# A four-layer graph network on one core: narrow sums of two turn pairs together, and the closing sums and products in another order

## The chip, the core and the metric

The kernel runs on one core of a Trainium2 chip. The time is that of the device in microseconds, from the first to the last instruction of one execution. Three runs of the kernel before gave a median of 811.44 us (811.31 to 813.11).

## What is computed

The input is a feature matrix `x` of 4096 nodes by 64, and a dense adjacency `adj` of 4096 by 4096 whose entries are 0 or 1 (about one in 128 is 1). Four layers follow each other, and each adds its result to `x`:

```
h = relu(layernorm(x));  x = x + layer_k(h, adj)      for k = 0, 1, 2, 3
```

Layer 0 weighs the neighbours of a node by their rank from the end, w = 0.5 ** (number of later neighbours), up to 100 of them, and computes `w @ (h @ W) + b`. Layer 1 is an attention with weights `adj * sigmoid(score)`. Layer 2 is a gated unit applied twice, each time with `m = adj @ (x @ W)`. Layer 3 is a weighted midpoint on a hyperbolic ball:

```
num = A @ (gamma * X);  den = A @ (gamma - 1);  alpha = sum(A, axis=1)
two_mean = num / den;   mid = tanh(0.5 * artanh(|two_mean|)) * direction
out = tanh(alpha * artanh(|mid|)) * direction        -> logmap, relu, expmap
```

## The kernel before, in words

**Tiling.** The nodes are 32 blocks of 128. The transposed adjacency is cut into four column quarters q of 1024, and so into 128 tiles of 128 x 1024. Each is loaded once, as one byte per entry, and kept for all layers (`A8`, names A...). Most are cast by the DMA that GpSimd issues (`load0`, L860), some come whole in float32 and are cast on chip (`cast0`). The program assumes that all entries are 0 or 1, and so every tile is loaded whole a second time, at whatever moment, and tested on VectorE (`checks`: `whole` with the sum of odd entries in `odd`). At the end one product of 128 x 1 (`flag_ps`) adds up what was found; where something was, a general kernel runs after this one. In this case it doesn't.

**Who sets the order.** The kernel is written as generators that yield operations, and a planner, `Weave`, issues them while the program is built. It keeps a clock for each engine (`self.t`), a cost for each operation (for instance 0.2 + 0.9e-3 n us on ScalarE, in `Engine.cost`), and the time at which each tile will be ready. The main streams (`stream0`, `stream1`, `layer2`, `layer3`) write TensorE's products in a fixed order. At each `weave.draw()` the planner puts in what fits from the waiting pieces: preparation of the next layer (`pre0` ... `pre3`, `post0` ... `post3`), and, as a background piece, the entry tests. While `weave.quiet` holds, no background piece is drawn. The engines then run what they were given, each in its own order; whatever the planner's clocks say, on the chip they wait by semaphores.

**Layer 0** (`stream0`). A turn takes one tile (block b, quarter q), b downwards from 31. `turn` multiplies the tile by a triangular matrix (`ftri`), after the earlier tile was multiplied by another one (`fupd`), and so keeps in two accumulator banks, `cnt0` and `cnt1` of 512 columns each, the number of later neighbours of each entry. ScalarE or VectorE reads each bank into `w` (times -128, relu, as int16: read as bfloat16 that is the weight). The first bank is always read by ScalarE, the second by ScalarE in turns of even b, by VectorE in turns of odd b from the twelfth turn on. The next turn's first product may go into a bank when it has been read. Two turns make a pair, and a pair's sums (`sums`) come two pairs or so later:

```
first turn | three wide sums | second turn | one wide sum, four narrow sums
```

The source of the sums, `h`, is split in three bfloat16 parts: two of them stand side by side in `hm` (128 columns, wide), the third in `lo` (64 columns, narrow: `add_lo`). A narrow sum uses one column half of the array; the sums for c = 0 and c = 1 use different halves.

**Layer 3** (`layer3`). The source `S3` is split in three parts again, so that one product of 128 x 196 gives all of them (`sum3`). The 4096 result nodes are eight parts u of 512. Accumulators have room for three parts, so parts 0, 1, 2 are first summed over the first half of the source blocks and set aside (`take3`), then 3, 4, 5 over all of them, in four quarters as the source gets ready; then the second half of 0, 1, 2; then 6 and 7. `post3` closes three parts at a time (6 and 7 singly): signs, lengths, artanh, tanh, relu, addition to `X`, store. It works on VectorE and ScalarE beside the sums. In its closing `between()` scales v by relu and the reciprocal length (names n<-n,ny in the profile), while the logarithm is computed; the result of tanh (rc) then scales v once more (n<-n,rc).

Of the kernel before, what the change touches and what calls it, by code (L numbers as in the profile page):

```python
# [13 lines left out]
ALU = mybir.AluOpType  # L14
# [555 lines left out]
NQ = 4  # L570
QB = 8
# [220 lines left out]
def fast_kernel(ctx: ExitStack, tc: tile.TileContext, t: dict, out: bass.AP, flag: bass.AP):  # L792
# [13 lines left out]
    NB = N // P  # L806
# [10 lines left out]
    weave = Weave()  # L817
# [314 lines left out]
    def stream0():  # L1132

        cols = [slice(c * CW, (c + 1) * CW) for c in (0, 1)]
        cnt, acc, waiting = [], {}, []

        def turn(q, b):

            n = q * NB + NB - 1 - b
            a = a8(q, b)  # L1140
            weave.at[A8[q][b // 2].tensor.name] = weave.at[A8[q][b // 2].tensor.name + "odd" * (b % 2)]
            wt = b2("w", (P, 2 * CW), I16)
            for c in (0, 1):
                if b < NB - 1:
                    before = a8(q, b + 1)(c)
                    mm(like(cnt[c], before), upd, before, start=False, stop=False)
                mm(like(cnt[c], a(c)), tri, a(c), start=b == NB - 1, stop=b == 0)

                if c == 0 or b % 2 == 0 or n < 12:
                    S_.activation(wt[:, cols[c]], cnt[c], AF.Relu, scale=-128.0)  # L1150
                else:
                    V.tensor_scalar(wt[:, cols[c]], cnt[c], -128.0, 0.0, op0=ALU.mult, op1=ALU.max)
            if n + 12 < len(tiles) and not direct(n + 12):
                load0(n + 12)
            if n + 12 < len(tiles) and direct(n + 12):
                load0(n + 12)
            for k in (1, n + 3):
                if k in whole:
                    cast0(k)
            return [wt[:, x].bitcast(BF16) for x in cols]  # L1160

        def sums():

            if not waiting:
                return
            q, b, w0, w1 = waiting[0]
            if b == NB - 1:
                acc[q] = [one(f"acc{c}") for c in (0, 1)]
            for c in (0, 1):
                add_hm(acc[q], 0, b, c, w0[c], b == NB - 1)  # L1170
            add_hm(acc[q], 0, b - 1, 0, w1[0], False)
            yield
            add_hm(acc[q], 0, b - 1, 1, w1[1], False)
            for i, wt in enumerate((w0, w1)):
                for c in (0, 1):
                    add_lo(acc[q], 0, b - i, c, wt[c], b - i == 0)
            waiting.pop(0)
            if b == 1:
                weave.add(post0(q, acc.pop(q)))

        def here(item):
            part = source(0, item[1])[0]
            return part in DONE and weave.ready("P", names(LO[part])) <= weave.t["P"]

        for q in range(NQ):
            cnt[:] = [two(f"cnt{c}")[:, :CW] for c in (0, 1)]
            for b in range(1, NB, 2)[::-1]:

                if len(waiting) > 3:
                    weave.until(source(0, waiting[0][1])[0], DONE)  # L1190
                first = second = iter(())
                if waiting and (len(waiting) > 3 or here(waiting[0])):
                    first = second = sums()
                w0 = turn(q, b)
                weave.draw()
                next(first, None)
                weave.draw()
                w1 = turn(q, b - 1)
                weave.draw()
                next(second, None)  # L1200
                weave.draw()
                waiting.append((q, b, w0, w1))
                if q == 0 and b in (NB - 1, NB - 3):
                    load_x((b - NB + 3) // 2, S_)
                    weave.add(pre0((b - NB + 3) // 2))
                if q == 0 and b == NB - 3:
                    weave.add(checks(), back=True)
                if q == 0 and b == NB - 9:
                    S_.dma_start(W, t["consts"][:, :L.at["scales"].stop])
                    weave.add(constants())  # L1210
                if len(waiting) > 2 and here(waiting[0]):
                    for _ in sums():
                        weave.draw()
                if b == NB // 2 + 1:
                    load_x(q, Y_)
                    if q == 0:
                        depth[0] = 2
                    if q == NQ - 1:
                        load1(0)
                        depth[0] = 2  # L1220
            for x in cnt:
                free(x)
        begin1()
        while waiting:
            for _ in sums():
                weave.draw()
# [459 lines left out]
    def layer3():  # L1686

        half = NB // 2
        sets = (0, 1, 2), (3, 4, 5)
        early = {}  # L1690
        for k in range(2):
            for place, u in enumerate(sets[0]):
                weave.until((4, k), DONE)
                sum3(u, place, k * QB, k * QB + QB)
                if k:
                    early[u] = take3(u)
        for lo, hi in ((0, 1), (1, 2), (2, 3), (3, 4)):
            for place, u in enumerate(sets[1]):
                weave.until((4, lo), DONE)
                sum3(u, place, lo * QB, hi * QB)  # L1700
                if hi == NQ:
                    summed(u, take3(u))
        weave.quiet = False
        while weave.back and weave.back[0][1].e == "D":
            weave.issue(weave.back[0])
        for place, u in enumerate(sets[0]):
            sum3(u, place, half, NB)
            summed(u, take3(u, early.pop(u)))
        for place, u in enumerate((6, 7)):
            sum3(u, place, 0, NB)  # L1710
            summed(u, take3(u), alone=True)
        while weave.back:
            weave.force(True)
        others = nc.values_load(flag)
        weave.finish()
        return others
# [31 lines left out]
    def post3(parts3):  # L1748

        nb = CB * len(parts3)
        sgn, den, ss = stat("sgn", nb), stat("den", nb), stat("ss", 2 * nb)
        part = [slice(i * CB, (i + 1) * CB) for i in range(len(parts3))]
        vs = [n65[:, :, :D] for u, (n65, al) in parts3]
        for h, v, (u, (n65, al)) in zip(part, vs, parts3):
            d = n65[:, :, D]
            yield DV.tensor_scalar(sgn[:, h], d, 0.0, 2.0, op0=ALU.is_ge, op1=ALU.mult)  # L1760
            yield DV.scalar_tensor_tensor(v, rows(sgn[:, h]), -1.0, v, op0=ALU.add, op1=ALU.mult)
            sq = b2("sq")
            yield AC.activation(sq[:, :CB, :], v, AF.Square)
            yield DV.scalar_tensor_tensor(sq[:, CB:, :], v, 0.0, v, op0=ALU.max, op1=ALU.mult)
            yield DV.tensor_scalar(den[:, h], d, -1.0, DEN_EPS, op0=ALU.mult, op1=ALU.max)
            yield DV.tensor_tensor(den[:, h], den[:, h], d, ALU.max)
            yield DV.tensor_reduce(ss.rearrange("p (k b) -> p k b", k=2)[:, :, h],
                                   sq.rearrange("p (k b) d -> p k b d", k=2), AX.X, ALU.add)
        yield from preload(AF.Ln)
        rd = yield from recip(den)  # L1770
        n, r = yield from lengths(ss)
        t = stat("t", nb)
        yield DV.tensor_tensor(t, n[:, :nb], rd, ALU.mult)
        ratio = stat("ratio", nb)

        def between():
            yield DV.tensor_tensor(ratio, n[:, nb:], r[:, :nb], ALU.mult)
            for h, v in zip(part, vs):
                yield DV.scalar_tensor_tensor(v, v, 0.0, rows(r[:, nb:][:, h]), op0=ALU.max, op1=ALU.mult)

        a = yield from artanh2(t, between())
        for h, (u, (n65, al)) in zip(part, parts3):
            yield DV.scalar_tensor_tensor(a[:, h], a[:, h], 0.25, al, op0=ALU.mult, op1=ALU.mult)
        yield DV.scalar_tensor_tensor(a, a, ARTANH_MAX, ratio, op0=ALU.min, op1=ALU.mult)
        yield AC.activation(a, a, AF.Tanh)
        for h, v, (u, (n65, al)) in zip(part, vs, parts3):
            yield DV.tensor_tensor(v, v, rows(a[:, h]), ALU.mult)
            x = X[u // 2][:, (u % 2) * CB:(u % 2 + 1) * CB, :]
            yield DV.tensor_tensor(x, x, v, ALU.add)
            yield SY.dma_start(out_nm[:, u * CB:(u + 1) * CB, :], x)  # L1790
# [103 lines left out]
```

## Time and profile before

| stretch, us | stage | TensorE busy | VectorE busy | ScalarE busy |
|---|---|---|---|---|
| 5 to 232 | layer 0 | 220.1 | 168.5 | 132.9 |
| 232 to 493 | layer 1 | 257.6 | 216.4 | 166.9 |
| 493 to 695 | layer 2, both steps | 200.2 | 167.1 | 53.3 |
| 695 to 790 | layer 3 with sums | 94.6 | 72.3 | 35.5 |
| 790 to 811 | closing without sums | 0.0 | 13.3 | 7.1 |
| whole span, 810.7 | | 772.4 (95%) | 638.3 (79%) | 396.9 (49%) |

A row of the profile gives the engine, the line, the operation, the names written and read (buffer numbers left out), the shape and how often. Nearly all lines are those of two helpers (L781 for VectorE, ScalarE and the DMA issues of the sync queue, L976 for products), so the names tell what it is: cnt is a count bank, acc an accumulator, hm and lo the source parts, whole an entry test or its load, n a part's numerator in layer 3. In an order of time a row gives start and length first; a bracket at its end tells how long the engine had been idle and who released it. A product's end is modelled: what counts is the distance of starts.

### The profile page before, as it was taken

What the parts mean: (1) busy time and instruction counts of PE and PEld (TensorE: products, weight loads), DVE (VectorE), ACT (ScalarE), POOL (GpSimd) and SP (SyncE); (2) the same over time, 40 slices, a digit from 0 to 9 for tenths busy, and PEclk for the clock granted to TensorE, in tenths of its full rate; (3) what the DMA queues carried; (4) which work ended last, traced back from release to release, by engine and by line L of the source; (5) the groups of instructions that cost most, each with busy time, mean ns of one, the idle gap of its engine ahead of it and who ended that gap; (6) DMA issues with size and microseconds to landing.
All of it is one profiled execution on the core that took longest, in us unless ns stands there. A gap on an engine that the chain in (4) does not pass through costs nothing.

```text
span 810.7 us, 12099 instructions
## 1 busy us (share of the span) xinstructions
PE 772.4 (95%) x4473; PEld 355.6 (44%) x4494; DVE 638.3 (79%) x1433; ACT 396.9 (49%) x613; POOL 60.9 (8%) x125
## 2 busy tenths in 40 slices
PE   5999999999999999999999999999999999999990
PEld 2334444444433323333333333444444354699990
DVE  6886777677678788888888888878788787774896
ACT  5655555565565657567666664022220244462333
POOL 3333233230000000000000000000000000000000
PEclk9999999999999999999999999999999999999995
DMA  9999999998301032022022007696888910000010
GB/s 221 151 178 168 202 160 190 197 160 188 108 14 40 0 113 71 0 73 84 0 66 78 13 1 255 240 323 234 293 289 317 326 38 1 2 2 2 1 37 21
DMA packets 43954, 98.39 MB, mean 121 GB/s; under 512 B 5104, under 2 KB 20464, under 8 KB 43888
## 3 DMA queue, kind: packets, MB, share of 16 engines
q1 hardware_dynamic: 25888, 78.98, 29.0%
q0 software_dynamic: 15840, 14.42, 19.0%
q10 hardware_dynamic: 2160, 4.14, 1.4%
q8 instruction: 37, 0.61, 0.3%
q14 instruction: 29, 0.24, 0.1%
HBM read 135.54 MB, written 5.24 MB: 174 GB/s over the span
## 4 chain that ended last, share of the span: by engine, by line
PE 85%; DVE 10%; issue 1%; ACT 1%; DMA 1%; SPq 0%; ACTq 0%; DVEq 0%
PE acc L976 51%; PE score L976 14%; PE cnt L976 13%; DVE n L781 2%; PE rz L976 2%; DVE sig L781 2%; PE ps_t L980 1%; PE ps_l L976 1%; DVE ss L781 1%; DMA whole<-in_adjT 1%; DVE nt L781 1%; PE ps_kq L976 1%; PE ih L976 1%; ACT sig L781 1%; PE ps_n L980 1%
## 5 line engine op out<-in xcount | busy, mean ns | idle before, releaser
L781 ACT ACTIVATE sig<-score,fatt_add,fatt_mul 128x1024 f32<-128x1024 f32 x128 | 148.1, 1200 | 86.9 <-PE score L976 86.3
L781 DVE TENSOR_TENSOR sig<-sig,A 128x1024 f32<-128x1024 f32 x128 | 151.5, 1221 | 40.2 <-ACT sig L781 39.5
L781 DVE SCALAR_TENSOR_TENSOR whole<-whole 128x1024 f32<-128x1024 f32 x128 | 153.1, 1219 | 6.0 <-DMA whole<-in_adjT 5.6
L781 ACT ACTIVATE w<-cnt 128x512 int16<-128x512 f32 x198 | 111.2, 595 | 89.8 <-PE cnt L976 88.5
L976 PE MATMUL score<-qd,kT 64*128 64x512 f32 x512 | 129.6, 623 | 0.0
L976 PE MATMUL acc<-sig,S 128*64 128x512 f32 x512 | 125.7, 608 | 1.5 <-DVE sig L781 1.4
L976 PE MATMUL acc<-A,hm 128*128 128x512 fp8e4 x512 | 115.7, 380 | 0.0
L976 PEld LDWEIGHTS <-hm 128*128 128x128 bf16 x768 | 73.4, 98 | 90.1 <-issue 10.0
L976 PE MATMUL cnt<-A,ftri 128*128 128x512 fp8e4 x256 | 97.7, 384 | 8.2 <-ACT A L781 8.0
L976 PE MATMUL cnt<-A,fupd 128*128 128x512 fp8e4 x248 | 95.5, 385 | 2.6 <-DVE w L781 1.5
L976 PE MATMUL acc<-S,A 128*128 128x196 bf16 x1024 | 88.2, 247 | 0.0
L976 PEld LDWEIGHTS <-A 128*128 128x128 fp8e4 x1024 | 87.1, 96 | 1.1 <-issue 0.8
L976 PEld LDWEIGHTS score<-qd,kT 64*128 64x128 f32 x512 | 44.0, 187 | 81.2 <-ACT sig L781 39.2
L781 DVE TENSOR_SCALAR w<-cnt 128x512 int16<-128x512 f32 x58 | 40.1, 691 | 45.4 <-PE cnt L976 41.0
L976 PE MATMUL acc<-w,hm 128*128 128x512 bf16 x235 | 71.0, 379 | 0.9 <-issue 0.2
L860 POOL DMA_DIRECT2D A<-in_adjT x110 | 59.2, 540 | 120.0 <-DMA A<-in_adjT 119.1
L976 PEld LDWEIGHTS acc<-sig,S 128*64 128x64 f32 x512 | 30.5, 136 | 83.5 <-issue 39.9
L976 PEld LDWEIGHTS <-lo 128*64 128x64 bf16 x768 | 36.8, 109 | 58.4 <-issue 36.2
L976 PE MATMUL acc<-A,lo 128*64 128x512 fp8e4 x512 | 59.2, 381 | 0.0
L781 ACT ACTIVATE mt<-acc 64x512 f32<-64x512 f32 x32 | 18.9, 591 | 67.6 <-PE acc L976 67.1
L976 PEld LDWEIGHTS <-fupd 128*128 128x128 bf16 x248 | 24.3, 98 | 46.1 <-issue 24.3
L1655 POOL MEMSET S<- 128x4 bf16 x8 | 0.9, 116 | 546.9 <-PE ps_l L976 502.2
(185 smaller groups left out, 640.1 us busy)
## 6 DMA issues: line engine op xcount, KB each, us to landing
whole<-in_adjT SPq DMA_DIRECT2D x128, 512.0 KB, 7.1
A<-in_adjT POOLq DMA_DIRECT2D x110, 128.0 KB, 13.6
qd<-qs SPq DMA_DIRECT2D x16, 128.0 KB, 2.8
mx<-gs SPq DMA_DIRECT2D x16, 128.0 KB, 8.1
xT<-gs SPq DMA_DIRECT2D x8, 256.0 KB, 7.3
x<-in_x SPq DMA_DIRECT2D x6, 256.0 KB, 6.5
xs<-x SPq DMA_DIRECT2D x4, 256.0 KB, 4.8
qs<-qT ACTq DMA_DIRECT2D x4, 256.0 KB, 6.4
```

What stands on the lines that cost most here:

```text
L781: return fn(*args, **kw)
L860: nc.gpsimd.dma_start(A8[q][b // 2][:, b % 2, :], a)
L976: nc.tensor.matmul(o, lhsT, rhs, start=start, stop=stop, skip_group_check=True)
L980: nc.tensor.transpose(o, src, ident)
L1655: nc.gpsimd.memset(S3[q, c][:, :, 3 * e:], 1.0)
```

## The change

There are three edits. **In layer 0** the narrow sums of a pair are held back until those of the next pair are due; then all eight follow each other. **In layer 3** the parts 3, 4, 5 are no longer summed quarter by quarter, all three each: parts 3 and 4 go through three quarters, then what is left of the entry tests is issued, and then each of the three parts is finished in one go, part 5 over its whole second half. **In the closing**, relu and the reciprocal length no longer scale v in an own product of 128 x 256; the reciprocal is multiplied into the small factor after tanh, and relu goes into the last product.

```diff
@@ stream0 @@
-        cnt, acc, waiting = [], {}, []
+        cnt, acc, waiting, narrow = [], {}, [], []
...
             add_hm(acc[q], 0, b - 1, 1, w1[1], False)
-            for i, wt in enumerate((w0, w1)):
-                for c in (0, 1):
-                    add_lo(acc[q], 0, b - i, c, wt[c], b - i == 0)
-            waiting.pop(0)
+
+            narrow.append(waiting.pop(0))
+            if len(narrow) == 2:
+                for q, b, *ws in narrow:
+                    for i, wt in enumerate(ws):
+                        for c in (0, 1):
+                            add_lo(acc[q], 0, b - i, c, wt[c], b - i == 0)
+                narrow.clear()
             if b == 1:
                 weave.add(post0(q, acc.pop(q)))
@@ layer3 @@
-        for lo, hi in ((0, 1), (1, 2), (2, 3), (3, 4)):
+        for k in range(2):
             for place, u in enumerate(sets[1]):
-                weave.until((4, lo), DONE)
-                sum3(u, place, lo * QB, hi * QB)
-                if hi == NQ:
-                    summed(u, take3(u))
+                sum3(u, place, k * QB, k * QB + QB)
+        for place, u in enumerate(sets[1][:2]):
+            weave.until((4, 2), DONE)
+            sum3(u, place, half, half + QB)
+
+        weave.until((4, NQ - 1), DONE)
         weave.quiet = False
         while weave.back and weave.back[0][1].e == "D":
             weave.issue(weave.back[0])
+        for place, u in enumerate(sets[1]):
+            sum3(u, place, half + QB if place < 2 else half, NB)
+            summed(u, take3(u))
@@ post3 @@
         def between():
             yield DV.tensor_tensor(ratio, n[:, nb:], r[:, :nb], ALU.mult)
-            for h, v in zip(part, vs):
-                yield DV.scalar_tensor_tensor(v, v, 0.0, rows(r[:, nb:][:, h]), op0=ALU.max, op1=ALU.mult)
...
         yield AC.activation(a, a, AF.Tanh)
+        yield DV.tensor_tensor(a, a, r[:, nb:], ALU.mult)
         for h, v, (u, (n65, al)) in zip(part, vs, parts3):
-            yield DV.tensor_tensor(v, v, rows(a[:, h]), ALU.mult)
+            yield DV.scalar_tensor_tensor(v, v, 0.0, rows(a[:, h]), op0=ALU.max, op1=ALU.mult)
```

## The prediction

> **What bounds the kernel now.** I read the stretches by stage first, then the page's groups, then the order of time in layer 0 and at the end. The answer by stretches (us; busy time of TensorE, weight loads, VectorE, ScalarE, GpSimd, then clock, DMA share, GB/s) has these rows for layer 0, layer 3 while TensorE runs (from 751 on beside the closing work), and what follows:
>
> ```profile
> 5.00:232.00 227.00, 220.05 (x1093) 93.09 (x1114) 168.50 (x406) 132.90 (x245) 56.13 (x105) 1.00 0.96 168
> 695.00:751.00 56.00, 56.00 (x624) 52.84 (x623) 36.63 (x135) 22.93 (x55) 0.46 (x4) 1.00 0.01 2
> 751.00:790.00 39.00, 38.61 (x454) 38.17 (x451) 35.63 (x148) 12.56 (x39) 0.00 (x0) 1.00 0.06 19
> 790.00:811.00 21.00, 0.00 (x0) 0.00 (x0) 13.25 (x70) 7.07 (x13) 0.00 (x0) 0.60 0.07 22
> ```
>
> TensorE sets the pace until 790, although DMA is at 0.96 in layer 0; a tail of 21 us has no matmul. From 751 VectorE is at 35.6 of 39 us: it enters the tail with a backlog. Two turns of layer 0, from the timeline (start, length, engine, line):
>
> ```profile
> 104.05 0.38 PE L976 MATMUL cnt<-A,ftri 128*128 128x512 fp8e4 x1
> 104.48 0.38 PE L976 MATMUL cnt<-A,ftri 128*128 128x512 fp8e4 x1
> 104.52 1.09 ACT L781 ACTIVATE w<-cnt 128x512 int16<-128x512 f32 x2 [1.82 <-PE cnt L976]
> 104.70 0.38 PE L976 MATMUL acc<-w,hm 128*128 128x512 bf16 x1
> 105.01 0.62 PE L976 MATMUL acc<-w,lo 128*64 128x512 bf16 x4
> 105.56 0.39 PE L976 MATMUL cnt<-A,fupd 128*128 128x512 fp8e4 x1
> 105.79 0.38 PE L976 MATMUL cnt<-A,ftri 128*128 128x512 fp8e4 x1
> ...
> 93.21 0.38 PE L976 MATMUL cnt<-A,fupd 128*128 128x512 fp8e4 x1 [0.56 <-ACT w L781]
> ```
>
> Starts of equal wide matmuls are 0.216 apart. Into the narrow sums it takes 0.31, their two column halves run beside each other (0.24 from pair to pair), out of them 0.31. So one narrow set costs 0.65 (104.70 to 105.56 is 0.865, less 0.216), and 0.22 of it is switching. The last row is of another turn: the next count product stood 0.56 behind ScalarE's reading of the same counts. In the tail, on VectorE:
>
> ```profile
> 751.82 0.88 DVE L781 TENSOR_TENSOR n<-n,acc 128x260 f32<-128x260 f32 x2 [2.22 <-ACT alpha L781]
> 752.62 1.22 DVE L781 SCALAR_TENSOR_TENSOR whole<-whole 128x1024 f32<-128x1024 f32 x1
> 755.31 0.16 DVE L781 TENSOR_SCALAR sgn<-n 128x4 f32<-128x4 f32 x1
> 768.36 0.42 DVE L781 SCALAR_TENSOR_TENSOR n<-n,ny 128x256 f32<-128x256 f32 x1
> 770.10 0.75 DVE L781 SCALAR_TENSOR_TENSOR n<-n,ny 128x256 f32<-128x256 f32 x2
> 789.36 0.42 DVE L781 SCALAR_TENSOR_TENSOR sq<-n 128x256 f32<-128x256 f32 x1
> 798.61 0.68 DVE L781 TENSOR_REDUCE ss<-sq 128x8 f32<-128x512 f32 x1
> 805.05 0.43 DVE L781 TENSOR_TENSOR X<-X,n 128x256 f32<-128x256 f32 x1
> ```
>
> TensorE ends near 789.5, VectorE at 805.5; the last store and its landing fill the rest to 810.7, some 5.2.
>
> [...]
>
> **Edit 1, narrow sums of two turn pairs together.** The TensorE order of the changed program has 123 mode switches in layer 0 before and 61 after. Only ordering changes: the same 1,084 products. Per four turns the doubled set gains two pairs of narrow sums, 2 x 0.24 = +0.48; the other pair loses its set, -0.65, and the slower first product behind it (0.226 for 0.216), together -0.66. That is -0.18, times 31 is -5.6, if nothing else waits.
>
> But the 0.65 covers something. The count bank must be read by ScalarE before the next turn's product may go on with it. With T the start of the bank's last product (104.05), ScalarE starts 0.42 to 0.47 later, as its two starts show here and elsewhere, and takes 0.597 (median of its w group): done at T+1.01 to T+1.07. Next product: T+0.05 after that, which is the distance I read where the product visibly waited (14.07 behind a reading that ended at 14.02; the same 0.05 at 93.21). So it cannot start before T+1.06 to T+1.12. Before, it starts at T+1.51. Without narrow sums nothing but one wide product lies there and it would be due at T+0.864: a stall of 0.20 to 0.26. The second bank is also ScalarE's in this turn (the second turn of a pair reads both there), done 0.49 later, at T+1.50 to T+1.56, so its product starts at T+1.55 to T+1.61 instead of the T+1.50 to T+1.56 that the stalled row would allow: +0.06 more. The stall is 0.26 to 0.32 and queued behind it are all further products of TensorE, so it lies on the path. Net per four turns: -0.18 + 0.26 to 0.32 = +0.08 to +0.14; I take 0.11. In the changed order 28 of the 31 pairs without narrow sums have only the one wide product there; 3 have two key/query products (about 0.86), which fill the gap, -0.18 each; the last two pairs save one more set of switches, -0.2. Sum: 28 x 0.11 - 3 x 0.18 - 0.2 = +2.4.
>
> Two smaller things. ScalarE and VectorE have other work between their readings (squares of 0.6, a table load of 1.28 at 91.16, entry tests of 1.22), and 0.45 of slack that hid it is gone in every second pair. And the planner sees the new gaps: it puts 43 entry tests into layer 0 instead of 36. VectorE's queue between two of its own readings holds more than a period in about as many places as before (the worst 3.4 us of work); so I add 0.8 for both, bounds 0 and 3. The later tests need 7 more tiles of 512 KB, but adjacency tiles land 4 us and more before use after turn 24 and over 20 after turn 78, so DMA costs nothing. Layer 0: **+3.2**.
>
> **Layers 1 and 2.** Their TensorE orders are nearly the same (148 switches become 146, 52 become 57): 5 - 2 = 3 switches of about 0.1, some +0.3, and I count 0 with bounds of 1 either way, as 5 tests leave VectorE, which TensorE hides. The flag product moves from layer 3 into layer 2: it waits for the tests' sum, and behind it stand wide sums; VectorE needs about 1.8 there, TensorE has 2.3 of work in front, so nothing.
>
> **Edit 2, leftover tests in front, and another order of the last sums.** In the changed order no test is left when layer 3 begins. Before, two of them with their sum stood between 752.62 and 755.31 on VectorE, ahead of the closing work: -2.7 for the backlog. The order of sums itself moves no product out: the 1,024 take as long. It asks for the last quarter's source one unit of 32 products earlier (32 x 0.085 = 2.7). That source was ready at 738.2, its first product ran at 743.1, so 4.9 of slack become 2.2: nothing.
>
> **Edit 3, folded product.** Each closing group of three loses three products of 128x256 (0.34 to 0.36 apart, together 1.07) and gains one of 128x12, 0.17 by its neighbours: -0.9, twice. The two single groups lose 0.35 and gain 0.2 behind tanh, where it isn't hidden: -0.1 each.
>
> **Sum of the tail.** The backlog falls by 2.7 + 1.8 = 4.5, of which a few waits for sums take 0.6: the single group's sq, at 789.36 before, comes at 785.5. Its chain (4.5) then ends at about 790, just as the last accumulator comes in (TensorE's end at 789.5 and 1.1 of evacuation). From there: flag load 0.3, rest of group 6's logarithm 1.7, its closing and the start of group 7 2.2, which puts the reduction of 798.61 at 794.8; from it to the end of X there were 6.87, now 6.8: 801.6 instead of 805.5. Tail **-3.9**; bounds -3 and -4.7 (all of the backlog and the single groups).
>
> **The rivals.**
> - Cancelling (chance 0.53): 811.4 + 3.2 - 3.9 = **810.7**. For it: the 0.05 and the readings' length, seen in many turns. Against: it rests on gaps that before has nowhere in just this form.
> - The grouping pays (0.28): ScalarE's reading hides or stalls are half as long; layer 0 gains 0 to 5.6 and the end comes at 807.5 to 801.9. For it: switches cost 0.22 wherever I looked. Against: T+0.864 lies before the reading's end.
> - Readings late (0.19), on the slower side: seven more tests of 1.22 each delay a reading by some 0.8, as two do before (at 30.1 and 47.2), +5.6, and the tail saves only the tests' 2.7: 811.4 + 2.4 + 5.6 - 2.7 = 816.7. For it: VectorE is at 168 of 227 us and gets more. Against: its queue is no fuller in the worst place.
>
> **How the numbers follow.** The predicted time is the first case's. Its own terms (0.08 to 0.14, 0 to 3, 1 either way, -3 to -4.7) spread it from 807.5 to 814; the range 806.5 to 815 takes in the nearer half of both rivals. Faster by over 0.3% (under 809.0): 0.32; within: 0.46; slower (over 813.9): 0.22.
>
> **What would show it.** In layer 0: count products that start 0.05 behind a ScalarE reading in every second pair, and a period of 6.6 for four turns instead of 6.5; layer 0 ending near 235. At the end: VectorE some 4 us nearer to TensorE's last product (12 instead of 16). Wrong it would be if the gap after the lone wide product is 0.216 (first rival), if VectorE's readings rather than ScalarE's end the waits (second), or if layers 1 and 2 shift by more than 1.

## The result and the profile after

The changed kernel takes **808.28 us** (median of 9 executions, 807.93 to 809.79) where the kernel before takes 812.11 (median of 9, 811.31 to 813.11): ratio 0.9959, 95% interval 0.9949 to 0.9968. That is 3.8 us less: inside the predicted range, 2.4 below the predicted 810.7, and just past the 0.3% that had been counted as no change.

Four of the nine traces here show a dip of TensorE's granted clock near 290 us, in layer 1, that costs some 1.6 us: layer 1 takes 257.57 to 257.69 in these four and 255.98 to 256.06 in the other five. The profile of before (span 810.7) has the dip and that of the changed kernel (806.1) has not, so 1.6 of the 4.6 between the two spans is not the change. The times of every version fall into two groups some 1.5 us apart; the traces with the dip are of executions in the upper group, those without it of the lower one, so about half of all executions seem to have it. The answer by short stretches shows it, first for before, then for the changed kernel (us; TensorE, weight loads, VectorE, ScalarE, GpSimd busy, clock, DMA share, GB/s):

```profile
292.00:293.00 1.00, 1.00 (x4) 0.57 (x6) 1.00 (x3) 0.54 (x1) 0.00 (x0) 0.71 0.08 16
293.00:294.00 1.00, 1.00 (x4) 0.34 (x2) 0.48 (x2) 0.40 (x1) 0.00 (x0) 0.50 0.52 78
294.00:295.00 1.00, 1.00 (x4) 0.00 (x0) 0.16 (x1) 0.80 (x1) 0.00 (x0) 0.50 0.67 172
295.00:296.00 1.00, 1.00 (x6) 0.32 (x6) 1.00 (x1) 0.69 (x1) 0.00 (x0) 0.58 0.96 375
```

```profile
290.00:295.00 5.00, 3.80 (x20) 1.82 (x22) 4.15 (x9) 2.51 (x4) 0.00 (x0) 1.00 0.41 112
```

The four microseconds of before lose 0.29, 0.50, 0.50 and 0.42 of full speed, 1.7 together; the changed kernel keeps 1.00. What is left between the two traces, stage by stage, from starts and ends of the same instructions:

| stage, from and to | before | changed | difference |
|---|---|---|---|
| layer 0, to its last narrow sum | 237.81 | 238.38 | +0.6 |
| layer 1, to its last sum | 257.63, less the dip of 1.6: 256.0 | 256.06 | 0.0 |
| layer 2, to the first sum of layer 3 | 200.39 | 199.97 | -0.4 |
| sums of layer 3, first to last | 93.53 | 93.66 | +0.1 |
| last sum to VectorE's end | 16.12 | 12.65 | -3.5 |

Together -3.2. Group by group the medians differ by about as much: 811.39 and 808.01 in the lower group, 812.74 and 809.74 in the upper one. All executions together give 3.8, because the median of before falls into its upper group and that of the changed kernel into its lower one.

TensorE's last sum, from which the tail is counted, in the timelines of before and of the changed kernel:

```profile
789.36 0.25 PE L976 MATMUL acc<-S,A 128*128 128x196 bf16 x1
788.07 0.25 PE L976 MATMUL acc<-S,A 128*128 128x196 bf16 x1
```

The stretches of the changed kernel, which answer to those shown of before:

```profile
5.00:232.00 227.00, 220.49 (x1106) 97.66 (x1107) 174.29 (x418) 132.97 (x244) 55.78 (x105) 1.00 1.01 184
695.00:751.00 56.00, 55.75 (x626) 52.95 (x625) 34.75 (x133) 21.94 (x55) 0.46 (x4) 1.00 0.01 2
751.00:790.00 39.00, 37.31 (x439) 37.08 (x437) 35.24 (x158) 14.74 (x41) 0.00 (x0) 1.00 0.07 22
790.00:811.00 21.00, 0.00 (x0) 0.00 (x0) 9.21 (x50) 4.77 (x10) 0.00 (x0) 0.63 0.05 16
```

VectorE has 5.8 us more in layer 0 (174.29 instead of 168.50), where six more entry tests of 1.22 now stand (43 instead of 36 in all of layer 0), and 4.0 less after 790. TensorE's busy time in layer 0 is nearly the same (220.49 instead of 220.05). Now the lone wide product of a pair without narrow sums, from the timeline of the changed kernel:

```profile
69.36 0.38 PE L976 MATMUL cnt<-A,ftri 128*128 128x512 fp8e4 x1
...
69.84 1.08 ACT L781 ACTIVATE w<-cnt 128x512 int16<-128x512 f32 x2 [0.36 <-PE cnt L976]
70.01 0.38 PE L976 MATMUL acc<-w,hm 128*128 128x512 bf16 x1
...
70.49 0.38 PE L976 MATMUL cnt<-A,fupd 128*128 128x512 fp8e4 x1
...
70.98 0.38 PE L976 MATMUL cnt<-A,fupd 128*128 128x512 fp8e4 x1
```

The bank's last product starts at 69.36, its reading 0.48 later, and the next product of that bank at 70.49, 0.48 behind the wide one where 0.216 would do: a wait of 0.26. The second bank adds 0.06 (70.98). The next product starts 0.051 behind the end of the reading. It is the same in nearly all pairs: 27 waits at the first bank (18 of 0.20 and 9 of 0.26, 5.96 together) and 22 at the second (1.41). The period of four turns is 6.58 (65.47 to 72.05) instead of 6.50. The long narrow set, in TensorE's timeline of the changed kernel:

```profile
66.64 1.05 PE L976 MATMUL acc<-w,lo 128*64 128x512 bf16 x8
67.63 0.39 PE L976 MATMUL cnt<-A,fupd 128*128 128x512 fp8e4 x1
```

Eight starts and the way out take 0.99; four and the way out took 0.55 (105.01 to 105.56). So two more pairs cost 0.43, not 0.48: only the first step from pair to pair is 0.24, each later one is 0.216 (the four pairs start at 66.64, 66.88, 67.10 and 67.31).

VectorE in the tail, by the timeline of the changed kernel:

```profile
750.75 0.88 DVE L781 TENSOR_TENSOR n<-n,acc 128x260 f32<-128x260 f32 x2 [4.93 <-ACT alpha L781]
751.56 0.16 DVE L781 TENSOR_SCALAR sgn<-n 128x4 f32<-128x4 f32 x1
...
784.29 0.42 DVE L781 SCALAR_TENSOR_TENSOR sq<-n 128x256 f32<-128x256 f32 x1
...
793.86 0.68 DVE L781 TENSOR_REDUCE ss<-sq 128x8 f32<-128x512 f32 x1
...
800.29 0.42 DVE L781 TENSOR_TENSOR X<-X,n 128x256 f32<-128x256 f32 x1
```

No test stands before the signs any more (751.56; in before 755.31, with two tests ahead), no n<-n,ny is left, and the single group's sq, at the time of the last sum in before (789.36), comes 3.8 ahead of the last sum (788.07).

### The profile page after: what moved, and what is told of

It is laid out like the page before. It is cut to its first block, busy times and chain, and to the rows that moved or that the text cites. A ratio compares the mean times of both kernels' runs of the same rounds, so it can differ in the third digit from the quotient of the medians.

```text
span 806.1 us, 12128 instructions
## 1 busy us (share of the span) xinstructions
PE 772.6 (96%) x4494; PEld 360.1 (45%) x4494; DVE 635.6 (79%) x1429; ACT 397.8 (49%) x613; POOL 60.6 (8%) x125
## 5 line engine op out<-in xcount | busy, mean ns | idle before, releaser
L976 PE MATMUL acc<-w,hm 128*128 128x512 bf16 x256 | 75.6, 379 | 0.0
L976 PEld LDWEIGHTS <-lo 128*64 128x64 bf16 x768 | 39.3, 109 | 51.2 <-issue 22.5
L976 PEld LDWEIGHTS <-ftri 128*128 128x128 bf16 x256 | 24.8, 98 | 47.2 <-issue 20.3
## 6 DMA issues: line engine op xcount, KB each, us to landing
xT<-gs SPq DMA_DIRECT2D x8, 256.0 KB, 7.2
x<-in_x SPq DMA_DIRECT2D x6, 256.0 KB, 6.2
xs<-x SPq DMA_DIRECT2D x4, 256.0 KB, 6.0
qs<-qT ACTq DMA_DIRECT2D x4, 256.0 KB, 6.0
```

Source lines behind the costliest of these rows:

```text
L976: nc.tensor.matmul(o, lhsT, rhs, start=start, stop=stop, skip_group_check=True)
```

## The experiments

The executions of before beside them gave 812.02 (20, first four kernels) and 812.77 (11, last three). "Layer 0" is the distance from the first count product with the triangular matrix of the second quarter to the last narrow sum; it is 176.30 in before and repeats to 0.01 between kernels that have the same layer 0. "Tail" is from the last sum to VectorE's end. "Lower group" is the median of the executions that seem to have no dip, and how many these are; it bears a comparison better than the median of all, since the share with the dip differs from kernel to kernel.

| kernel | median, us | lower group, us | ratio to before (95%) | layer 0 | tail | tests after the first sum of layer 3 |
|---|---|---|---|---|---|---|
| before | 812.11, 812.02, 812.77 | 811.39 (4 of 9), 811.29 (10 of 20), 811.38 (3 of 11) | | 176.30 | 16.12 | 2, at 752.6 |
| changed | 808.28 | 808.01 (5 of 9) | 0.9959 (0.9949 to 0.9968) | 176.90 | 12.65 | none |
| edit 1 alone | 810.65 | 809.54 (5 of 11) | 0.9978 (0.9969 to 0.9987) | 176.89 | 14.05 | none |
| edits 2 and 3 | 807.88 | 807.79 (3 of 5) | 0.9952 (0.9939 to 0.9966) | 176.31 | 12.57 | 2, at 736.5 |
| edit 3 alone | 811.02 | 810.24 (4 of 8) | 0.9982 (0.9971 to 0.9993) | 176.30 | 15.24 | 2, at 753.2 |
| edit 2 alone | 810.72 | 809.30 (3 of 7) | 0.9972 (0.9961 to 0.9984) | 176.30 | 14.05 | 2, at 738.2 |
| before, two tests left out | 809.13 | 809.09 (4 of 6) | 0.9967 (0.9955 to 0.9979) | 176.31 | 14.13 | none |
| changed, wide sums 2 and 2 | 807.23 | 805.31 (1 of 5) | 0.9931 (0.9917 to 0.9945) | 175.36 | 12.66 | none |
| changed, wide sums 3, 0, 3, 2 | 803.32 | 802.51 (2 of 4) | 0.9894 (0.9878 to 0.9909) | 172.68 | 12.65 | none |

### Edit 1 alone

```diff
+            narrow.append(waiting.pop(0))
+            if len(narrow) == 2:
+                for q, b, *ws in narrow:
...
```

> The kernel before with edit 1 alone (narrow sums of two pairs together). My theory: the switches saved (some 0.22 us for each of 31 pairs, -6.8) and the stalls behind the lone wide product (27 at the first bank, 22 at the second, together 7.4 in the trace of the changed kernel) cancel, so 0 to +1 us against before: some 812.7 where before has 812.1. The period of four turns is 6.58 to 6.59 instead of 6.50, and the end of VectorE stays some 16 us after the last product. Rival: the grouping pays, and the 1.6 us by which layer 1 is shorter in the changed kernel belong to it as well: 809 to 810.5.

Neither was right as a whole. Layer 0 went as the theory said: +0.6 and the period of four turns of the changed kernel. But the whole came out 1.4 below before, and the tail is 2.1 shorter although nothing of layer 3 was touched. VectorE's timeline at the first closing group of this kernel shows why:

```profile
751.02 0.88 DVE L781 TENSOR_TENSOR n<-n,acc 128x260 f32<-128x260 f32 x2 [2.21 <-ACT alpha L781]
751.82 0.16 DVE L781 TENSOR_SCALAR sgn<-n 128x4 f32<-128x4 f32 x1
```

The signs follow the evacuation at once; the two tests are gone. The planner, which sees the new gaps in layer 0, places seven tests more there, and so none is left over for layer 3: those seven are the two of layer 3 and five of layer 2's second step. Grouping pays through the entry tests, not through TensorE's time in layer 0.

### Edits 2 and 3 without edit 1

```diff
-            narrow.append(waiting.pop(0))
-            if len(narrow) == 2:
-                for q, b, *ws in narrow:
-                    for i, wt in enumerate(ws):
-                        for c in (0, 1):
-                            add_lo(acc[q], 0, b - i, c, wt[c], b - i == 0)
-                narrow.clear()
+            for i, wt in enumerate((w0, w1)):
+                for c in (0, 1):
+                    add_lo(acc[q], 0, b - i, c, wt[c], b - i == 0)
+            waiting.pop(0)
```

> The changed kernel without edit 1 (each pair does its own narrow sums again; edits 2 and 3 stay). My theory: layer 0 is as before, the tail as in the changed kernel: 0 to 1 us below the changed kernel, some 807.7 (before 812.1, changed 808.3). Rival: the grouping gives part of the gain, so this one is 1.5 to 3 us above the changed kernel, 809.8 to 811.

807.88, as the theory said, and its interval overlaps that of the changed kernel. Edit 1 is worth nothing measurable beside the other two: in the traces it costs 0.6 in layer 0 and gains 0.4 in layer 2, and what it gains alone in the tail, edit 2 gains as well.

### Edit 3 alone

```diff
-            for h, v in zip(part, vs):
-                yield DV.scalar_tensor_tensor(v, v, 0.0, rows(r[:, nb:][:, h]), op0=ALU.max, op1=ALU.mult)
...
+        yield DV.tensor_tensor(a, a, r[:, nb:], ALU.mult)
```

> The kernel before with edit 3 alone (the closing product folded). My theory: each closing group of three has three products of 128x256 less and one of 128x12 more on VectorE, -0.9 us each, twice, and VectorE's backlog is what the end waits for: -1.5 to -1.8, some 810.4. Rival: a wait for an accumulator or for ScalarE takes its place: 0 to -0.5, 811.6 to 812.1.

It lies between the two: the tail is 0.9 shorter, not 1.5 to 1.8. With the tests out of the way the same edit is worth more: edits 2 and 3 against edit 2 alone 1.5 (14.05 to 12.57), the changed kernel against edit 1 alone 1.4 (14.05 to 12.65). The work removed is the same each time; what differs is how long VectorE then waits. In the trace of edit 3 alone it waits twice for the tanh of a group of three, 0.20 each, where before has no wait in these places; with edits 2 and 3 there is one such wait, of 0.20, and edit 2 alone already has one of 0.28. That is 0.4 of what is missing. The rest was not separated.

### Edit 2 alone

```diff
-        for lo, hi in ((0, 1), (1, 2), (2, 3), (3, 4)):
...
+        while weave.back and weave.back[0][1].e == "D":
+            weave.issue(weave.back[0])
+        for place, u in enumerate(sets[1]):
+            sum3(u, place, half + QB if place < 2 else half, NB)
+            summed(u, take3(u))
```

> The kernel before with edit 2 alone (leftover tests in front, last sums in another order). My theory: the two tests and their sum, 2.7 us, leave VectorE's backlog, of which 0.3 to 0.6 is lost in waits: -2.1 to -2.4, some 809.9; with edit 3 alone this adds up to the 3.5 us by which the tail of the changed kernel is shorter. Rival: the order of the last sums itself brings the gain (a source asked for at another moment, accumulators free sooner), and it is -3 or more, with the groups of VectorE at other distances from TensorE's end than the 2.7 explain.

The tail is 14.05, 2.1 shorter, as the theory said. The median, 810.72, is 0.8 above the expected 809.9, since four of the seven executions are of the upper group; in the lower one it is 2.0 less than before. The tests are still there, but earlier, in VectorE's timeline of this kernel:

```profile
738.15 1.22 DVE L781 SCALAR_TENSOR_TENSOR whole<-whole 128x1024 f32<-128x1024 f32 x1
739.30 1.22 DVE L781 SCALAR_TENSOR_TENSOR whole<-whole 128x1024 f32<-128x1024 f32 x1
```

Between 741 and 752 VectorE mostly waits for accumulators there (7.2 us of idle time in front of its n<-n,acc), so the tests cost nothing at 738, where in before they hold the closing work up at 752. It is the same 14.05 as with edit 1 alone, by another way.

### Before, two entry tests left out

Two tiles are not tested in this kernel.

```diff
-        todo = [(b, q) for n, (q, b) in enumerate(tiles) if not direct(n)]
+        todo = [(b, q) for n, (q, b) in enumerate(tiles) if not direct(n)][:-2]
```

> The kernel before, with the last two entry tests left out (these two tiles are not tested). My theory: in the kernel before two tests and their sum stand ahead of the closing work on VectorE, and edit 1 alone and edit 2 alone both gain by taking them out of there, 2.07 us between last product and VectorE's end; so leaving them out gives the same 14.0 to 14.1 us after the last product instead of 16.1, and 2 us less, some 810. Layer 2 keeps its wait of 1.1 us behind a table load near 676. Rival: it is the order of the last sums, or the sums' own place, that gains: then the end stays some 16 us behind the last product.

The tail is 14.13, with the old order of sums. So the tests' place is the whole gain of edit 2, and of edit 1 in the tail; the order of the last sums brings nothing by itself. TensorE's wait near 676 stayed as expected (below).

### The changed kernel with two and two wide sums

In a pair that has no narrow sums, the third wide sum moves from the first gap to the second.

```diff
+            if narrow:
+                add_hm(acc[q], 0, b - 1, 0, w1[0], False)
             yield
+            if not narrow:
+                add_hm(acc[q], 0, b - 1, 0, w1[0], False)
             add_hm(acc[q], 0, b - 1, 1, w1[1], False)
```

> The changed kernel, but a pair without narrow sums has two wide sums after each of its turns (2 and 2) instead of 3 and 1. The products and the mode switches stay the same. My theory (the next count product waits for the reading of its bank, which is done 1.06 to 1.12 us after the bank's last product began, plus 0.05): the first bank's wait in the lone pair falls from 0.20 or 0.26 to 0 to 0.04, the second bank's stays 0.05 to 0.1 behind ScalarE and comes up in the pair's first turn, behind VectorE's longer reading (0.08 to 0.14). Per pair 0.13 to 0.24 instead of 0.27: 1 to 4 us below the changed kernel, some 806 where it has 808.3. Rival: what limits there is how much work ScalarE and VectorE have in a period of two turns; then the wait only moves, and the time is that of the changed kernel, 808 to 808.6.

807.23 is 1.0 below the changed kernel, the lower end of what the theory allowed; but four of the five executions are of the upper group. By the traces it is 2.1 faster, with the dip's 1.6 taken off: 1.7 in layer 0 and 0.4 in layer 2. (The 1.06 to 1.12 of this expectation already holds the 0.05.) Its timeline, in a pair without narrow sums:

```profile
68.58 0.69 DVE L781 TENSOR_SCALAR w<-cnt 128x512 int16<-128x512 f32 x1 [2.39 <-PE cnt L976]
...
69.33 0.38 PE L976 MATMUL cnt<-A,fupd 128*128 128x512 fp8e4 x1
...
70.19 0.38 PE L976 MATMUL cnt<-A,fupd 128*128 128x512 fp8e4 x1
```

The wait behind ScalarE is gone (the product at 70.19 stands 0.216 behind the wide one), and one behind VectorE has come up in the first turn: VectorE's reading takes 0.69 instead of 0.60, and the product at 69.33 starts 0.05 behind it, 0.15 late. All waits at count banks sum to 8.6 in this trace and to 10.3 in that of the changed kernel; the difference is the 1.7 by which all of layer 0 is shorter (236.66 against 238.38).

### The changed kernel with three, none, three, two

```diff
             yield
-            add_hm(acc[q], 0, b - 1, 1, w1[1], False)
+            if late:
+                add_hm(*late.pop())
+            last = acc[q], 0, b - 1, 1, w1[1], False
+            if narrow and b > 1:
+                late.append(last)
+            else:
+                add_hm(*last)
```

> The changed kernel, but one wide sum of the pair that does eight narrow ones is put off into the next pair: the wide sums after four turns are 3, 0 (with the eight narrow ones), 3, 2 instead of 3, 1, 3, 1. Same products, same switches. My theory: the wait of 0.27 in each lone pair falls to 0.05 to 0.10, and the long set covers its own gap without the wide sum; in 24 of 28 places that is 4 to 5 us less than the changed kernel, some 804. The end after the last product stays 12.6. Rival: the period is limited elsewhere (readings of VectorE, DMA, or work of ScalarE), and the time stays at 807 to 808.6.

**803.32: 1.1% faster than before (interval 1.2% to 0.9%) and the fastest of all here.** Layer 0 is 4.2 shorter than in the changed kernel over three quarters, 5.7 over all four (232.67 against 238.38). The same place in its timeline:

```profile
104.72 0.38 PE L976 MATMUL cnt<-A,ftri 128*128 128x512 fp8e4 x1
...
105.20 1.09 ACT L781 ACTIVATE w<-cnt 128x512 int16<-128x512 f32 x2 [0.36 <-PE cnt L976]
105.37 0.59 PE L976 MATMUL acc<-w,hm 128*128 128x512 bf16 x2
...
105.85 0.38 PE L976 MATMUL cnt<-A,fupd 128*128 128x512 fp8e4 x1
...
106.33 0.38 PE L976 MATMUL cnt<-A,fupd 128*128 128x512 fp8e4 x1
```

With the second wide product in the gap the count product starts 1.13 behind the bank's last one, as in the changed kernel (69.36 to 70.49), but 0.216 of that is now filled: 0.04 of wait is left, and 0.06 at the second bank. Where eight narrow sums stand, they cover the gap without a wide one: the count product at 66.14 starts 0.31 behind the last pair of them (65.83), which is the step out of a narrow set where nothing waits. Waits at count banks fall from 10.3 to 4.7, by 5.6, which is the gain. The products and the switches are those of the changed kernel; only the place of 28 wide sums differs.

## Why the prediction was right or wrong

**The sum: in the range, but the case it was built on did not come.** The 810.7 rests on layer 0 giving back 3.2 of the 3.9 that the tail gains. Layer 0 gave back 0.6 of 3.5. That the time is in the range is no proof of the sum: the range took in the nearer half of the rival "the grouping pays", and 808.28 lies nearer to that rival's 807.5 than to 810.7; a time under 809.0 had been given a chance of 0.32. What was right is the mechanism in layer 0 and the size of the tail.

**Layer 0: mechanism right, size too high (+3.2 predicted, +0.6 measured).** The wait behind ScalarE's reading came as described: 0.05 behind the reading, in the pairs with one wide product, period 6.58. Three terms of the sum were mis-sized, all in one direction:

- The saving, -0.18 for each of 31 pairs. The term "2 x 0.24 = +0.48" took the step seen in a set of two pairs for all steps; later steps are 0.216, so the two pairs cost 0.43 and the saving is 0.225. 31 x 0.045 = 1.4.
- The wait, 28 x 0.29 = 8.1 in the middle of the bounds. The first bank waited in 27 places, more often 0.20 than 0.26; the second in 22, as the gaps of the other five are filled by four transposes each: 5.96 + 1.41 = 7.4. That is 0.7.
- The 0.8 for disturbances. Waits of other kinds were 2.66 in before and are 2.9: 0.3. That is 0.5.

Together 2.6, the whole miss. What lay close to zero, +0.11 for a group of four turns, was the difference of two numbers of 0.2 and 0.3, so an error of 0.045 in one of them became 1.4 us.

**The tail: size right within its bounds (-3.9 predicted, -3.5 measured), one cause put to the wrong edit.** The prediction said that in the changed order no test is left when layer 3 begins, and booked the 2.7 under edit 2. It was edit 1 that had removed them, as edit 1 alone shows; the two tests are worth 2.0 to 2.1 there, whichever edit takes them away, not 2.7 less a small wait. Edit 2 had nothing to put in front in the changed kernel. Edit 3, put at 1.8 for its two groups of three, gave 1.4 to 1.5 on top. So the sum 4.5 - 0.6 came out as 2.1 + 1.4. The backlog itself fell as predicted: the single group's sq came 3.8 ahead of the last sum (predicted 3.9), and from the reduction at 793.86 to VectorE's end it took 6.85 (predicted 6.8). The missing 0.4 lies between the two.

That the new order of sums costs and brings nothing was right, shown by the kernel with two tests left out: the old order with its tail of 14.13 against 14.05 of edit 2.

**Layers 1 and 2: 0 predicted; 0.0 and -0.4 measured.** Within the bounds, but the reason given, that TensorE hides the tests, missed one place. In before, ScalarE's table load stands between the gate's products and the reading of r in layer 2's second step, and TensorE waits for that reading, as the timeline of before shows:

```profile
675.24 1.28 ACT L781 ACT_TABLE_LOAD   x1 [2.80 <-PE rz L976]
676.54 0.69 ACT L781 ACTIVATE r<-rz,gate_b 128x512 f32<-128x512 f32 x1
...
677.28 1.08 PE L976 MATMUL rz<-mx,g 128*64 128x512 f32 x4 [1.14 <-ACT r L781]
```

In the changed kernel ScalarE's timeline has the load three us ahead of the reading:

```profile
671.70 1.28 ACT L781 ACT_TABLE_LOAD   x1 [1.39 <-DVE ss L781]
...
674.67 0.69 ACT L781 ACTIVATE r<-rz,gate_b 128x512 f32<-128x512 f32 x1 [1.69 <-PE rz L976]
```

The 1.14 is gone there, in edit 1 alone, and in the kernel with two and two; it is present in all kernels with the old layer 0, and in the one with 3, 0, 3, 2, which has as many tests in layer 2 as before (73; the others 67 or 68). So the wait goes with how many tests the planner has left for this step; that the tests themselves decide on which side the load falls was not tried. Of the 1.14, 0.4 arrives at the start of layer 3; where the rest goes was not followed.

**The rivals.** "The grouping pays" was wrong in its reason (ScalarE's readings are not shorter, 0.597 in the median of both kernels; layer 0 gains nothing), though its direction was right; the time of the whole could not have told it from the first case, the experiments and the waits in layer 0 do. "Readings late" was wrong: the waits for VectorE's readings did not grow (1.98 in before, 1.8 in the changed kernel).

## What to carry to other kernels

When work is taken out of a gap, ask what the gap hid: here the narrow sums hid the reading of a count bank, and grouping them saved 7.0 and cost 7.4 until one wide product per four turns was moved into the emptied gap. A planner that fills gaps turns a change in one stage into a change of the backlog in another, so a part's gain has to be measured with it alone and without it; two edits that each shorten the tail by 2.1 may shorten it by no more together. Where an estimate is a small difference of two costs, get the larger terms from the very shape that will run (a set of eight, not of four), or give the range their error times the count.

## What the runs showed that was not expected

- Pairs of column halves step by 0.24 only once in a set; after that by 0.212 to 0.216, the pace of full products.
- Where ScalarE is free, the reading of a bank starts 0.416 or 0.476 behind the start of the bank's last product, with hardly anything between. The wait behind it is thus 0.20 or 0.26.
- The dip of the clock is half speed for 3.41 us: in before the granted clock is 0.50 from 292.42 to 295.83 (0.29 + 0.50 + 0.50 + 0.42 us lost). The other three traces with a dip, of edit 2 alone, edit 3 alone and two and two, lose 1.71 us each as well. In before it begins 1.8 us after the longest pause of TensorE in layer 1: 288.21 to 290.58, 2.38 from start to start, of which 1.79 is idle time in front of a transpose of k that waits for VectorE.
- The same pause stands in the changed kernel, 288.79 to 291.17 with 1.79 of idle time, and the clock keeps 1.00 there; so the pause alone does not bring the dip. In both traces the moments in the record of the clock lie whole numbers of 3.413 us apart: the changes at 292.42, 295.83 and 794.18 in before (1 and 146 steps), the record's beginning at 14.41 and the change at 792.65 in the changed kernel (228 steps). From the beginning of the pause to the next product that is no transpose it is 3.13 us in both. In before (288.80 to 291.93) 2.92 of this lie in the one step that ends where the dip begins; in the changed kernel (289.38 to 292.51) a step ends at 290.89, inside the pause, and no step holds more than 1.62 of it. That this place decides between 1.6 us and nothing is the author's reading of the traces and was not tried by an edit: no kernel without the pause was run.
